# Graph attention over gathered neighbours: lists of the first half made inside layer 1, four tiles in the first phase

## The chip, the cores and the metric

The kernel runs on one core of a Trainium2 chip. Its time is the device time of one execution in microseconds; of several executions the median counts. The core has a matrix engine (TensorE, PE in the profile; its weight loads are PEld), a vector engine (DVE), a scalar engine (ACT), GpSimd (POOL) and SyncE (SP), which issues loads and stores. ACT and POOL issue transfers too. Each engine works its own instructions in order.

## What is computed

Two graph layers over x (4096 x 512) and a sparse weighted adjacency adj (4096 x 4096, symmetric in its pattern, some 0.8% of it above zero, the diagonal among them):

```python
# layer 0
h = max(layernorm(x), 0)
d = rowsum(adj) ** -0.5
x = x + relu((d[:, None] * adj * d[None, :]) @ h @ W0 + b0)
# layer 1
h = max(layernorm(x), 0)
e = leaky_relu((h @ W @ a[:512]) + (h @ W @ a[512:]).T, 0.2)
att = softmax(where(adj > 0, e, -1e12), axis=1)
neg = -softmax(where(adj > 0, -e, -1e12), axis=1)
x = x + elu(concat([att @ h, neg @ h], axis=1) @ wtrans)
```

Layer 0 needs adj as a dense matrix. Layer 1 needs only its pattern, so it works on lists of neighbours.

## The kernel before, in words

**Layer 0, phase 1 (L921 to L983).** Rows come in 32 blocks of 128, columns of the result too. For each row block j the kernel loads the 128 rows of adj for their sums (`load_adj`, L660, four transfers of 512 KB), loads the same rows of the transposed adj for the first group's columns (`load_at`, L840), turns and projects h_j with W0 on PE (`project`, L679, eight PE records of 128x512), scales it by d (L702, ACT) to y_j, and multiplies: `multiply` (L852) adds adj times y_j into one accumulator (a PSUM bank) for every block of `GROUPS[0]`, here six blocks, 26 to 31. A product of floats shows as two PE records. y_j stays in SBUF for the rest of layer 0.

**Layer 0, phase 2 (`group`, L1032).** The remaining 26 blocks follow in groups of four or two, in the order of `GROUPS`. In sixteen steps jp each group loads its part of the transposed adj, makes sums of sub-blocks on DVE (`sum_at`, L880 to L883), and multiplies with seven products in place of eight (`multiply_blocks`, L893, 128x256 records). Within a step stand, in the order in which they are written: the multiply, `pack` (the mask bits of the same columns, ACT L716 or DVE L718, stored to `table` by POOL at L727), `finish0` for a block of the group before (x1, the next layer's h, and eight stores of the row into the eight copies of `table`, most from ACT's queue, L443), and the function `step`, which works off pieces of list making. A group's accumulators are taken over (`evict`, `join_blocks`, L776) at the beginning of the next group.

`EARLY` names groups whose masks are made earlier than the group itself, from columns loaded once more: (24,2) in group 2, (12,4) in group 3, (8,4) in group 4. A group in `EARLY` makes no masks of its own.

**Lists.** For every 64-row block layer 1 needs a list of neighbours: the rows of `table` that are gathered. `make_lists(g)` makes them for one half of the blocks (g=1: blocks 16 to 31, g=0: blocks 0 to 15). `make_keys` (L544) compares flags on DVE, transposes them with eight small PE transposes (L552) and makes keys on DVE. Then come 60 rounds of DVE's max and match_replace (`list_round`, L391, L393), each giving eight more entries; after 21, 39 and 60 rounds a list of one of three classes is complete and DVE turns it into row numbers (`li`, L406). 24 `join`s (L413), eight per class, put them into a DRAM tile with indirect transfers by POOL; all write the same tile, so each waits until the one before has landed. `deal` (L425) loads the finished lists into SBUF in three transfers. The pieces are queued in the Python lists `listing` and `joining`, and `step` takes up to two or three rounds and one join per step. Before, g=1 starts in group 3 and g=0 in group 5, both in layer 0.

**Transition.** The last group (24,2) shares its time with the first pair of layer 1, which starts on rows that are finished by then. `judge` (L1008) compares counts on DVE, and lets a dense version of layer 1 run instead if a list overflowed.

**Layer 1 (`sparse_layer1`).** 32 pairs of 64-row blocks, in the order 16 to 31, then 0 to 15. For each pair POOL gathers 22 tiles of 128 rows (L451; chunks a = 0, 1, 2 with 8, 6 and 8 of them) with the indices that `deal` left. A row holds 512 values of h, one of the scores, and 128 words of mask bits. For each block DVE and ACT make the weights: scores (L463, L469), exp of both signs (ACT, L473), mask (L482), sums (L487 to L493). PE then multiplies (`product`, L1296, 28 records of 128x512), DVE and ACT scale, PE turns (L508), and every second block `finish1` multiplies with wtrans (L1319, 16 records), and adds x1. The loop over k is written out so: product of block k, gathers for a block ahead (chunk 0 for even k, chunks 1 and 2 for odd), weights of block k+2, turn of block k-1, finish of an earlier pair. Tiles of gathered rows have six slots, two pairs' worth, so a gather waits until PE has used the pair two before (POOL g L451 <- PE u L1296 in the waits).

Of the kernel before, what the change touches and what calls it, by code (L numbers as in the profile page):

```python
# [19 lines left out]
P = 128  # L20
IB = 512


GROUPS = ((26, 6), (16, 4), (20, 4), (0, 4), (4, 4), (8, 4), (12, 4), (24, 2))

EARLY = {(24, 2): (2,), (12, 4): (3,), (8, 4): (4,)}
PAIR0 = 16
Y_PARTS = (8, 11, 13)
T_PARTS = (7, 9)
# [230 lines left out]
def gcn_gat_kernel(  # L260
# [251 lines left out]
            nc.scalar.copy(ut[:, g, :, (r % 2) * RB : (r % 2 + 1) * RB], tp[:, :, g, :])  # L512


    late_mask = ctx.enter_context(sbuf(name="late_mask", bufs=1, side="right"))
    late_m = late_mask.tile([P, EJ, TT * P], U8, name="late_m")
    with sbuf(name="y0", bufs=1) as y_pool, sbuf(name="wa", bufs=1) as wa_pool, sbuf(name="bits", bufs=4) as bits_pool, sbuf(name="small0", bufs=4) as small, ExitStack() as rest, ExitStack() as lists:
        list_pool = lists.enter_context(sbuf(name="list", bufs=1, side="right"))
        rank = list_pool.tile([P, EN], F32, name="rank")
        nc.gpsimd.iota(  # L520
            rank, [[-1, EN]], base=EN, channel_multiplier=0, allow_small_or_imprecise_dtypes=True
        )
        before = list_pool.tile([P, NE + 1, NH], F32, name="before")
        nc.gpsimd.memset(before[:, 0, :], 0.0)
        for e in range(NE):
            nc.vector.tensor_tensor(
                before[:, e + 1, :], before[:, e, :], ident[:, e * NH : (e + 1) * NH], ALU.add
            )
        start = list_pool.tile([NH, 1], F32, name="start")
        nc.gpsimd.iota(  # L530
            start, [[0, 1]], base=0, channel_multiplier=STR, allow_small_or_imprecise_dtypes=True
        )
        flags = [list_pool.tile([P, EJ * NE, 2 * NH], BF16, name=f"flags{g}") for g in range(2)]
        keys, lst = {}, {}

        b_bc = wa_pool.tile([P, F], F32, name="b_bc")
# [214 lines left out]
            nc.vector.scalar_tensor_tensor(y, acc, d_all[:, j : j + 1], b_bc, ALU.mult, ALU.add)  # L751
            return y

        def new_y(work, j, k):
            if k < 0:
                return work.tile([P, F], F32, tag="y", name=f"y{j}", bufs=4)
            if k == 0:
                spare.append(make_pool.tile([P, 3, F], F32, tag="keys", name="spare"))
            return spare[0][:, k]

        def evict(i0, acc, work, _):

            return {
                i0 + k: affine(new_y(work, i0 + k, k - 3), a, i0 + k) for k, a in enumerate(acc)
            }

        def join_blocks(i0, n, acc, work, new_w):

            ys = {}
            for x in range(n // 2):  # L770
                p16, p23, p45, p7 = acc[x]
                j0, j1 = i0 + x, i0 + n // 2 + x
                ys[j0], ys[j1] = y, v = [new_y(work, j, -1) for j in (j0, j1)]
                w = new_w(f"w{j0}")[:, :H]
                nc.vector.tensor_copy(y[:, :H], p16[:, :H])
                nc.vector.tensor_tensor(w, p16[:, H:], y[:, :H], ALU.add)  # L776
                nc.vector.tensor_tensor(y[:, H:], p45[:, H:], w, ALU.add)

                def first(p23=p23, y=y):
                    nc.vector.tensor_tensor(y, p23, y, ALU.add)  # L780

                def second(p7=p7, w=w, p45=p45, v=v):
                    two = "p (a f) -> p a f"
                    nc.vector.tensor_tensor(w, p7, w, ALU.add)
                    nc.vector.tensor_tensor(
                        v.rearrange(two, a=2),
                        p45.rearrange(two, a=2),
                        w.unsqueeze(1).to_broadcast([P, 2, H]),
                        ALU.add,
                    )  # L790

                if n == 2:
                    first()
                    affine(y, y, j0)
                    second()
                    affine(v, v, j1)
                else:
                    second()
                    first()
            if n > 2:  # L800
                for j, y in ys.items():
                    affine(y, y, j)
            return ys
# [178 lines left out]
                pack(bits6, i0, j, ats.pop(j), j < 2)  # L982
                mark()  # L983
        pending = (GROUPS[0], partial(evict, i0, acc))
        listing, joining, spare = [], [], []

        def make_lists(g):
            make_keys(g)
# [12 lines left out]
                if r + 1 == CAPS[c] // 8:  # L1001
                    listing.append(partial(rows_and_joins, c))

        def judge():


            ok = small.tile([P, 8], F32, tag="ok", name="ok", bufs=1)
            nc.gpsimd.memset(ok, 1.0)  # L1008
            nc.vector.tensor_tensor(listed, listed, count, ALU.is_equal)
            for g in range(2):  # L1010
                nc.vector.tensor_reduce(ok[:, 4 + g : 5 + g], listed[:, g], AX.X, ALU.min)
            nc.vector.tensor_tensor(room[0], room[0], room[1], ALU.min)
            nc.vector.tensor_scalar(ok[:NH, 0:1], room[0], 0.0, None, ALU.is_ge)
            nc.vector.tensor_reduce(ok[:, 1:2], d_all, AX.X, ALU.min)
            nc.vector.tensor_scalar(ok[:, 1:2], ok[:, 1:2], 0.0, None, ALU.is_gt)
            for g, vec in enumerate((s_all, t_all)):
                sq = small.tile([P, NJ], F32, tag="sq", name=f"sq{g}", bufs=1)
                nc.vector.tensor_tensor(sq, vec, vec, ALU.mult)
                nc.vector.tensor_reduce(ok[:, 2 + g : 3 + g], sq, AX.X, ALU.max)
                nc.vector.tensor_scalar(  # L1020
                    ok[:, 2 + g : 3 + g], ok[:, 2 + g : 3 + g], MAXS * MAXS, None, ALU.is_le
                )
            bad = small.tile([P, 1], F32, tag="bad", name="bad", bufs=1)
            nc.vector.tensor_reduce(bad, ok[:, 0:7], AX.X, ALU.min)
            nc.vector.tensor_scalar(bad, bad, 0.0, None, ALU.is_equal)
            bad_ps = bank("bad_ps")
            nc.tensor.matmul(bad_ps[0:1, 0:1], bad, ones[:, 0:1], start=True, stop=True)
            verdict = const.tile([1, 1], I32, name="verdict")
            nc.vector.tensor_copy(verdict, bad_ps[0:1, 0:1])
            return verdict  # L1030

        def group(b, work, at_pool, sum_pool, step, prod, n_h=2):  # L1032
# [2 lines left out]
            i0, n = GROUPS[b]  # L1035
            nj = 8 // n
            (p0, pn), take = pending
            order = [p0 + k for k in ((0, 2, 1, 3) if b > 1 else range(pn))]
            ats, sums = {}, {}

            def prepare(jp):
# [12 lines left out]
            for jp in range(NP):  # L1054
# [8 lines left out]
                        for x in range(n // 2)  # L1063
                    ]
                multiply_blocks(acc, n, jp, ats[jp], sums[jp])
                if (i0, n) not in EARLY:
                    pack(bits_pool, i0, 2 * jp, ats[jp])
                for (e0, m), when in EARLY.items():
                    if b in when:
# [21 lines left out]
        with sbuf(name="work0", bufs=2) as work, sbuf(name="sums", bufs=3) as sum_pool, sbuf(name="at", bufs=6) as at_pool:  # L1091

            def prod(name):
                return work.tile([P, F], F32, tag="q", name=name, bufs=1)

            for b in range(1, len(GROUPS) - 1):

                def step(jp):
                    if jp == 2 and b in (3, 5):
                        make_lists((1, 0)[b == 5])  # L1100
                    for _ in range((2, 3)[b == 6] if jp != 2 else 0):
                        if listing:
                            listing.pop(0)()
                    if joining:
                        joining.pop(0)()

                group(b, work, at_pool, sum_pool, step, prod)
            while listing:
                listing.pop(0)()
            while joining:  # L1110
                joining.pop(0)()
        lists.close()
        late = ctx.enter_context(sbuf(name="late", bufs=1, side="right"))
        late_h = late.tile([P, n_late, ROW_W], F32, name="late_h")
        ut0 = late.tile([P, 2, FC, P], F32, name="ut0")
        s_pair = late.tile([P, P], F32, name="s_pair")
# [2 lines left out]
        with sbuf(name="work2", bufs=2) as work, sbuf(name="sums2", bufs=2) as sum_pool, sbuf(name="at2", bufs=4) as at_pool, sbuf(name="scratch", bufs=1) as scratch, sbuf(name="pair", bufs=1) as pair:  # L1119
# [94 lines left out]
                        nc.scalar.activation(warm, ones[:, 0:1], AF.Sqrt)  # L1214
                    )

            group(len(GROUPS) - 1, work, at_pool, sum_pool, step, row_tile, 4)
            k = late0 % EJ
            nc.gpsimd.dma_start(
                out=rows_of(tab0, late0 // EJ)[:, k : k + n_late, ROW_W:],  # L1220
# [9 lines left out]
                late_weights0(r)  # L1230
            for r in blocks:
                late_product0(r)
            verdict = judge()


    def sparse_layer1():
        with ExitStack() as pools:

            def pool(name, bufs):
# [3 lines left out]
            slots = ((0, 0), (1, 0), (1, 2), (1, 1), (0, 1), (0, 2))  # L1243
            g_pools = {s: pool("g%d%d" % s, 1) for s in slots}
            tmp, small, p_pool = pool("tmp", 1), pool("small1", 2), pool("p", 3)
            work, ut_pool, wt_pool = pool("work1", 2), pool("ut", 2), pool("wt", 1)
            warm = small.tile([P, 1], F32, tag="warm", name="warm", bufs=1)
            nc.scalar.activation(warm, sign, AF.Exp)
            wt_sb = wt_pool.tile([P, 2 * FC, F], F32, name="wt_sb")
            s_pool = pool("s", 2)  # L1250
            gath, wgt, us, uts, srow = {}, {}, {}, {PAIR0: ut0}, {}

            def load_s(k):
# [106 lines left out]
            for k, r in enumerate(order):  # L1360
# [5 lines left out]
                if k + 4 - k % 2 < len(order):  # L1366
                    for a in ((0,), (1, 2))[k % 2]:
                        gather1(order[k + 4 - k % 2] // 2, a)
                if k + 2 < len(order):
                    weights(order[k + 2])  # L1370
                    if wanted and order[k + 2] % 8 == 7:
# [2 lines left out]
                    turn(order[k - 1])  # L1374
                if k == 2:
                    finish1(PAIR0)
                if k % 2 and k > 1:
                    finish1(order[k - 3] // 2)
            turn(order[-1])
# [43 lines left out]
```

## Time and profile before

| | us |
|---|---|
| median of 3 executions | 2135.89 (2132.7 to 2136.31) |
| the profiled execution, its own time | 2098.72 |
| its span | 2096.8 |
| phase 1, last multiply | 334.3 |
| phase 2, first to last L893 | 334.3 to 1030.2 |
| transition and first blocks of layer 1 | to about 1180 |
| mean granted PE clock | 0.981 |

The groups of phase 2, first to last product on PE (L893), from the trace:

| group | us | |
|---|---|---|
| (16,4) | 98.8 | |
| (20,4) | 97.0 | |
| (0,4) | 107.1 | list rounds, g=1 |
| (4,4) | 115.3 | joins, g=1 |
| (8,4) | 107.5 | list rounds, g=0 |
| (12,4) | 109.0 | joins, g=0 |
| (24,2) | 55.1 | |

In the lines of the profile, times are in us from the span's start unless a column says ns. A line of the groups names the line of the program, the engine, the operation, what it writes and reads, the count, then busy time and mean ns, then the idle time of the engine ahead of it and what ended that. A line of the waits reads: who waited, for whom, us in all, times, longest. "SPq" is SyncE's queue of transfers. In the table by stretches, each engine has its busy us and its number of instructions; PEclk is the granted TensorE clock, DMA share how busy the 16 DMA engines were.

### The profile page before, as it was taken

Reading aid. Unit: us, or ns where it says so; the run is one execution under the profiler, and the core shown is the slowest. Engines: PE = TensorE matmul, PEld = TensorE weight load, DVE = VectorE, ACT = ScalarE, POOL = GpSimd, SP = SyncE. Lnnn points to the kernel's source line nnn. Section 1 sums busy time; section 2 is a strip of 40 time slices with the busy share of each in tenths; the row PEclk is TensorE's granted clock in tenths of the full one; section 3 lists DMA queues with packets and bytes.
Section 4 is the critical chain, followed back from the end, with each engine's and each line's share of the span. In section 5 each row is a group of like instructions: output and inputs, shape, how many; then the busy total and the mean of one; then the engine's idle time right before and its main releaser. Section 6 shows DMA issues by size and latency. Waiting matters only on the chain.

```text
span 2096.8 us, 20037 instructions
## 1 busy us (share of the span) xinstructions
PE 1996.2 (95%) x6456; PEld 1180.1 (56%) x6456; DVE 1120.1 (53%) x2805; ACT 511.3 (24%) x876; POOL 917.0 (44%) x980
## 2 busy tenths in 40 slices
PE   7999999999899879899879999999999999999998
PEld 3444446888787768788634444444444444444443
DVE  5444436563798458945545455554544544445441
ACT  4645612222332310000111222212212211121120
POOL 2010001111113320220577777777777777776740
PEclk9999999999999999999989999999999999999999
DMA  9988927887887776383689888888888888888850
GB/s 381 366 307 321 371 71 252 290 284 220 307 281 256 253 222 238 90 270 111 204 265 302 255 288 293 263 287 254 271 240 274 261 258 245 242 247 236 240 161 22
DMA packets 188040, 524.11 MB, mean 250 GB/s; under 512 B 25235, under 2 KB 34419, under 8 KB 187926
## 3 DMA queue, kind: packets, MB, share of 16 engines
q0 software_dynamic: 71296, 275.22, 42.2%
q1 hardware_dynamic: 86640, 192.78, 27.1%
q10 hardware_dynamic: 29990, 54.75, 7.4%
q8 instruction: 52, 0.85, 0.2%
q14 instruction: 62, 0.51, 0.1%
HBM read 430.83 MB, written 102.92 MB: 255 GB/s over the span
## 4 chain that ended last, share of the span: by engine, by line
PE 49%; DVE 6%; DMA 5%; POOL 3%; issue 2%; ACTq 1%; ACT 0%; DVEq 0%; SPq 0%; POOLq 0%
PE u L1296 32%; PE o L1319 10%; PE p L893 5%; POOL g L451 3%; DMA g<-table,idx 2%; DVE keys L393 1%; PE tp L508 1%; DVE lst L391 1%; DMA table<-h 1%; DMA ld<-li,off 1%; DMA at<-in_adj_t 1%; PE u L1174 1%; ACTq L443 1%; DVE prod L816 0%; DMA table<-m 0%
## 5 line engine op out<-in xcount | busy, mean ns | idle before, releaser
L451 POOL DMA_INDIRECT g<-table,idx x704 | 747.8, 1062 | 259.9 <-issue 186.4
L1296 PE MATMUL u<-g,p 128*128 128x512 f32 x1736 | 762.4, 596 | 9.8 <-DVE p L482 9.8
L1296 PEld LDWEIGHTS u<-g,p 128*128 128x128 f32 x1736 | 326.0, 191 | 397.5 <-issue 362.9
L463 DVE TENSOR_TENSOR z<-g,s 128x512 f32<-128x512 f32 (+1 forms) x124 | 77.5, 625 | 390.4 <-DMA g<-table,idx 357.8
L893 PE MATMUL p<-t,sums 128*128 128x256 f32 x832 | 249.0, 384 | 13.3 <-DVE sums L881 13.3
L893 PE MATMUL p<-y,sums 128*128 128x256 f32 x832 | 252.0, 385 | 6.5 <-DVE sums L883 6.5
L893 PE MATMUL p<-y,at 128*128 128x256 f32 x832 | 252.4, 386 | 4.9 <-DMA at<-in_adj_t 4.6
L1319 PE MATMUL o<-wt_sb,ut 128*128 128x512 f32 x512 | 225.1, 592 | 0.5 <-ACT ut L512 0.5
L473 ACT ACTIVATE p<-z 128x896 f32<-128x896 f32 (+2 forms) x136 | 116.1, 905 | 268.3 <-DVE z L469 248.1
L893 PEld LDWEIGHTS p<-t,sums 128*128 128x128 f32 x832 | 159.6, 193 | 37.5 <-DVE sums L881 15.5
L893 PEld LDWEIGHTS p<-y,sums 128*128 128x128 f32 x832 | 160.7, 193 | 29.9 <-DVE sums L883 7.3
L852 PE MATMUL acc<-y,at 128*128 128x512 f32 x384 | 174.9, 593 | 2.4 <-ACT y L702 2.4
L482 DVE SCALAR_TENSOR_TENSOR p<-g,p 128x384 f32<-128x384 uint8 (+1 forms) x256 | 143.2, 620 | 63.3 <-ACT p L473 62.3
L893 PEld LDWEIGHTS p<-y,at 128*128 128x128 f32 x832 | 159.3, 193 | 30.7 <-ACT m L716 5.0
L727 POOL DMA_DIRECT2D table<-m x71 | 54.3, 766 | 248.5 <-ACT m L716 145.5
L1319 PEld LDWEIGHTS o<-wt_sb,ut 128*128 128x128 f32 x512 | 94.8, 190 | 107.8 <-issue 106.9
L716 ACT ACTIVATE m<-at 128x1024 uint8<-128x1024 f32 (+1 forms) x110 | 105.2, 987 | 183.8 <-DMA at<-in_adj_t 137.3
L893 PE MATMUL p<-t,at 128*128 128x256 f32 x416 | 126.3, 386 | 18.5 <-DVE w L776 17.7
L1305 ACT ACTIVATE us<-u,rl 128x512 f32<-128x512 f32 x62 | 42.5, 686 | 414.7 <-issue 217.4
L679 PE MATMUL yp<-w_sb,hx_t 128*128 128x512 f32 x256 | 123.2, 627 | 17.3 <-ACT y L702 14.8
L852 PEld LDWEIGHTS acc<-y,at 128*128 128x128 f32 x384 | 70.5, 190 | 80.5 <-issue 77.4
L413 POOL DMA_INDIRECT ld<-li,off x48 | 43.2, 901 | 159.8 <-DMA ld<-li,off 115.8
(182 smaller groups left out, 1718.5 us busy)
## 6 DMA issues: line engine op xcount, KB each, us to landing
at<-in_adj_t SPq DMA_DIRECT2D x136, 512.0 KB, 5.1
ar<-in_adj SPq DMA_DIRECT2D x128, 512.0 KB, 8.4
table<-h ACTq DMA_DIRECT2D x182, 258.0 KB, 5.8
table<-m POOLq DMA_DIRECT2D x55, 256.0 KB, 5.6
at<-in_adj_t SPq DMA_DIRECT2D x32, 384.0 KB, 5.0
g<-table,idx POOLq DMA_INDIRECT x704, 4.3
xr<-in_x SPq DMA_DIRECT2D x32, 256.0 KB, 3.5
x<-x1d SPq DMA_DIRECT2D x32, 256.0 KB, 5.2
```

The source lines that it names most:

```text
L413: return nc.gpsimd.indirect_dma_start(out=lst_dram[g][:, :], out_offset=bass.IndirectOffsetOnAxis(ap=off[g][:, e, c : c + 1], axis=0), in_ ...
L451: nc.gpsimd.indirect_dma_start(out=gt[:, k, :], out_offset=None, in_=table[2 * n // RPT], in_offset=bass.IndirectOffsetOnAxis(ap=idx[n // ...
L463: return nc.vector.tensor_tensor(z, t.to_broadcast([P, n, RB]), s.unsqueeze(1).to_broadcast([P, n, RB]), ALU.add)
L473: i = nc.scalar.activation(p[:, :, g, :], z, AF.Exp, scale=(1.0, -1.0)[g])
L482: nc.vector.scalar_tensor_tensor(e, m, 0.0, e, ALU.is_gt, ALU.mult)
L679: nc.tensor.matmul(yp, hx_t[j][:, c * P : (c + 1) * P], w0_sb[:, c, :], start=c == 0, stop=c == FC - 1,)
L716: nc.scalar.activation(m, at, AF.Sign)
L727: nc.gpsimd.dma_start(out=rows_of(t, e)[:, c:, ROW_W + (a - t * TT) * P // 4 : ROW_W + (b - t * TT) * P // 4], in_=masks[i0][:, c:, (a - i ...
L852: nc.tensor.matmul(a, at[:, 0, it * P : (it + 1) * P], y0[j], start=j == 0, stop=j == NJ - 1)
L893: i = nc.tensor.matmul(out, left[:, x * P : (x + 1) * P], right, start=jp == 0 and first, stop=jp == NP - 1 and (final or not first),)
L1296: nc.tensor.matmul(u, p[:, k0 + k].rearrange("p g c -> p (g c)"), gt[:, k, :F].bitcast(F32), start=k0 + k == 0, stop=k0 + k == nk - 1,)
L1319: nc.tensor.matmul(po, ut[:, g, c, :], wt_sb[:, g * FC + c, :], start=g == 0 and c == 0, stop=g == 1 and c == FC - 1,)
```

## The change

Six things, which belong together:

- `GROUPS` begins with (28,4) in place of (26,6): four accumulators in phase 1, and a new group (26,2) in phase 2, third in the order.
- `EARLY` keeps (24,2) alone. The groups (12,4) and (8,4) make their masks from their own columns.
- g=1 is listed in group 4, which is (0,4) as before. g=0 is listed within layer 1: after block k=3 of its loop the memory of the late rows is closed, a pool and the tables for the lists are made, and `make_lists(0)` follows. From k=4 on each k takes five pieces of `listing` and one of `joining`, and one more of `joining` follows each of the gather chunks 0 and 2.
- `judge` stands at k=40 in layer 1.
- The pool of s in layer 1 is made ahead of that of wt, so it lies elsewhere in SBUF. Flags of g=0 have a pool of their own.
- The first group's accumulators are evicted to four y tiles, without the spare tile.

```diff
-GROUPS = ((26, 6), (16, 4), (20, 4), (0, 4), (4, 4), (8, 4), (12, 4), (24, 2))
-
-EARLY = {(24, 2): (2,), (12, 4): (3,), (8, 4): (4,)}
+GROUPS = ((28, 4), (16, 4), (26, 2), (20, 4), (0, 4), (4, 4), (8, 4), (12, 4), (24, 2))
+
+EARLY = {(24, 2): (3,)}
...
-                if (i0, n) not in EARLY:
+                if (i0, n) not in EARLY and 2 * jp % nj == 0:
                     pack(bits_pool, i0, 2 * jp, ats[jp])
...
-                    if jp == 2 and b in (3, 5):
-                        make_lists((1, 0)[b == 5])
-                    for _ in range((2, 3)[b == 6] if jp != 2 else 0):
+                    if jp == 2 and b == 4:
+                        make_lists(1)
+                    for _ in range(2 if jp != 2 else 0):
                         if listing:
                             listing.pop(0)()
...
-            verdict = judge()
...
-            work, ut_pool, wt_pool = pool("work1", 2), pool("ut", 2), pool("wt", 1)
+            work, ut_pool, s_pool, wt_pool = pool("work1", 2), pool("ut", 2), pool("s", 2), pool("wt", 1)
...
-            s_pool = pool("s", 2)
...
                     for a in ((0,), (1, 2))[k % 2]:
                         gather1(order[k + 4 - k % 2] // 2, a)
+                        if a != 1 and joining:
+                            joining.pop(0)()
                 if k + 2 < len(order):
                     weights(order[k + 2])
...
                 if k == 2:
                     finish1(PAIR0)
+
+                if k == 3:
+                    lates.close()
+                    make_pool = pool("make1", 1)
+                    rank, before, start = list_tables(make_pool)
+                    make_lists(0)
+                if k > 3:
+                    for work_left, n in ((listing, 5), (joining, 1)):
+                        for todo in work_left[:n]:
+                            todo()
+                        del work_left[:n]
+                if k == 40:
+                    verdict = judge(small)
```

`list_tables` is the code that made `rank`, `before` and `start` ahead of layer 0 (L519 to L532), now a function that is called a second time.

More of the change, by code (lines that the diff above doesn't have):

```diff
@@ L512, in turn_u @@
             nc.scalar.copy(ut[:, g, :, (r % 2) * RB : (r % 2 + 1) * RB], tp[:, :, g, :])
-    late_mask = ctx.enter_context(sbuf(name="late_mask", bufs=1, side="right"))
+    flag_pools, lates = (ctx.enter_context(ExitStack()) for _ in range(2))
+    flag_pool = flag_pools.enter_context(sbuf(name="flags", bufs=1, side="right"))
+    flags = [flag_pool.tile([P, EJ * NE, 2 * NH], BF16, name="flags0")]
+    late_mask = lates.enter_context(sbuf(name="late_mask", bufs=1, side="right"))
     late_m = late_mask.tile([P, EJ, TT * P], U8, name="late_m")
@@ L518, in gcn_gat_kernel, with list_tables @@
         list_pool = lists.enter_context(sbuf(name="list", bufs=1, side="right"))
[L519 to L527, printed above, removed]
-            )
[L529 to L533, printed above, removed]
+        flags.append(list_pool.tile([P, EJ * NE, 2 * NH], BF16, name="flags1"))
+        def list_tables(pool):
+            rank = pool.tile([P, EN], F32, name="rank")
+            nc.gpsimd.iota(
+                rank,
+                [[-1, EN]],
+                base=EN,
+                channel_multiplier=0,
+                allow_small_or_imprecise_dtypes=True,
+            )
+            before = pool.tile([P, NE + 1, NH], F32, name="before")
+            nc.gpsimd.memset(before[:, 0, :], 0.0)
+            for e in range(NE):
+                nc.vector.tensor_tensor(
+                    before[:, e + 1, :], before[:, e, :], ident[:, e * NH : (e + 1) * NH], ALU.add
+                )
+            start = pool.tile([NH, 1], F32, name="start")
+            nc.gpsimd.iota(
+                start,
+                [[0, 1]],
+                base=0,
+                channel_multiplier=STR,
+                allow_small_or_imprecise_dtypes=True,
+            )
+            return rank, before, start
+        rank, before, start = list_tables(list_pool)
         keys, lst = {}, {}
@@ L752, in affine, with new_y @@
             return y
[L754 to L759, printed above, removed]
+        def new_y(work, j):
+            return work.tile([P, F], F32, tag="y", name=f"y{j}", bufs=4)
         def evict(i0, acc, work, _):
             return {
-                i0 + k: affine(new_y(work, i0 + k, k - 3), a, i0 + k) for k, a in enumerate(acc)
+                i0 + k: affine(new_y(work, i0 + k), a, i0 + k) for k, a in enumerate(acc)
             }
@@ L772, in join_blocks @@
                 j0, j1 = i0 + x, i0 + n // 2 + x
-                ys[j0], ys[j1] = y, v = [new_y(work, j, -1) for j in (j0, j1)]
+                ys[j0], ys[j1] = y, v = [new_y(work, j) for j in (j0, j1)]
                 w = new_w(f"w{j0}")[:, :H]
@@ L984, in gcn_gat_kernel @@
         pending = (GROUPS[0], partial(evict, i0, acc))
-        listing, joining, spare = [], [], []
+        listing, joining = [], []
+        verdict = None
         def make_lists(g):
@@ L1002, in make_lists, with judge @@
                     listing.append(partial(rows_and_joins, c))
-        def judge():
+        def judge(small):
             ok = small.tile([P, 8], F32, tag="ok", name="ok", bufs=1)
@@ L1037, in group @@
             (p0, pn), take = pending
-            order = [p0 + k for k in ((0, 2, 1, 3) if b > 1 else range(pn))]
+            order = [p0 + k for k in ((0, 2, 1, 3) if b > 1 and pn == 4 else range(pn))]
             ats, sums = {}, {}
@@ L1112, in gcn_gat_kernel @@
         lists.close()
-        late = ctx.enter_context(sbuf(name="late", bufs=1, side="right"))
+        late = lates.enter_context(sbuf(name="late", bufs=1, side="right"))
         late_h = late.tile([P, n_late, ROW_W], F32, name="late_h")
@@ L1215, in step @@
                     )
-            group(len(GROUPS) - 1, work, at_pool, sum_pool, step, row_tile, 4)
+            group(len(GROUPS) - 1, work, at_pool, sum_pool, step, row_tile, 3)
             k = late0 % EJ
@@ L1232, in gcn_gat_kernel @@
                 late_product0(r)
-            verdict = judge()
     def sparse_layer1():
+        nonlocal make_pool, rank, before, start, verdict
         with ExitStack() as pools:
```

## The prediction

> **What bounds the kernel now.** I read the page's totals first, then the busy times by stage, then the waits, then single rows of the timeline. The page says that TensorE (PE) is busy nearly throughout, and which groups are concerned:
>
> ```profile
> span 2096.8 us, 20037 instructions
> PE 1996.2 (95%) x6456; PEld 1180.1 (56%) x6456; DVE 1120.1 (53%) x2805; ACT 511.3 (24%) x876; POOL 917.0 (44%) x980
> ...
> L451 POOL DMA_INDIRECT g<-table,idx x704 | 747.8, 1062 | 259.9 <-issue 186.4
> ...
> L413 POOL DMA_INDIRECT ld<-li,off x48 | 43.2, 901 | 159.8 <-DMA ld<-li,off 115.8
> ```
>
> By stage (0 to 334 phase 1; then the groups of layer 0; from 1180 layer 1):
>
> ```profile
> core 0: us, PE busy (x) PEld busy (x) DVE busy (x) ACT busy (x) POOL busy (x), PEclk, DMA share, GB/s
> ...
> 25.00:250.00 225.00, 207.98 (x532) 94.32 (x533) 105.90 (x328) 129.04 (x272) 23.57 (x38) 0.97 0.94 347
> 250.00:334.00 84.00, 84.00 (x217) 37.27 (x216) 32.70 (x85) 22.64 (x40) 3.90 (x7) 1.00 0.40 133
> 334.00:530.00 196.00, 194.22 (x900) 169.84 (x899) 110.76 (x321) 51.18 (x70) 29.90 (x54) 1.00 0.82 271
> 530.00:638.00 108.00, 101.49 (x481) 87.74 (x480) 96.78 (x299) 36.08 (x41) 20.02 (x31) 0.97 0.87 291
> 638.00:753.00 115.00, 101.90 (x450) 87.40 (x449) 61.42 (x171) 31.62 (x37) 38.86 (x50) 0.94 0.77 249
> ...
> 1180.00:2097.00 917.00, 908.25 (x2367) 419.71 (x2365) 431.63 (x799) 182.52 (x308) 623.58 (x587) 1.00 0.78 240
> ```
>
> PE is full where no lists are made (334 to 530) and loses 6 to 13 us per group where DVE makes lists or POOL joins them. Layer 1 loses nothing: PE sets it, POOL (68% busy, plus issue gaps) is second. The waits say who leads whom in phase 1, in the joins and in layer 1:
>
> ```profile
> SPq L840 <- PE acc L852: 116.5, 19, 9.6
> ```
> ```profile
> POOL ld L413 <- DMA ld<-li,off: 115.8, 41, 5.9
> ...
> POOL g L451 <- PE u L1296: 54.9, 47, 3.4
> ```
>
> In phase 1 the load queue waits for PE, not PE for it. A join waits for the landing of the one before. Joins in a quiet stretch (POOL's timeline; the bracket is the idle time before):
>
> ```profile
> 853.87 0.88 POOL L413 DMA_INDIRECT ld<-li,off  x1 [3.14 <-DMA ld<-li,off]
> 857.42 0.83 POOL L413 DMA_INDIRECT ld<-li,off  x1 [2.67 <-DMA ld<-li,off]
> 859.64 0.83 POOL L413 DMA_INDIRECT ld<-li,off  x1 [1.38 <-DMA ld<-li,off]
> ```
>
> And how far layer 1's weights lie ahead of PE: the masks of its sixth block end at 1145.61+2.23=1147.8, the block's product starts at 1158.0.
>
> ```profile
> 1145.61 2.23 DVE L482 SCALAR_TENSOR_TENSOR p<-g,p 128x384 f32<-128x384 uint8 x4 [0.41 <-ACT p L473]
> ```
> ```profile
> 1158.03 2.39 PE L1296 MATMUL u<-g,p 128*128 128x512 f32 x5
> ```
>
> Measured so for every block, this lead is 10 us at block 5, 12 at 6, 17 at 10, 20 at 13, 24 at 19, and stays at 28 from block 23.
>
> **What the Trainium skill says.** "DMA: Bandwidth & Descriptors", Anatomy of one DMA: a POOL-issued DMA has a fixed cost of about 2 us, mostly the confirmation of its write. The trace agrees: joins land 1.9 us after issue at best, 3.3 in the median, 7.1 at worst. "SBUF — State Buffer", Who interferes with whom: a DVE instruction with one SBUF input, outside the two-port modes, doesn't hold up GpSimd. The trace agrees for the list rounds: joins beside L393 take 0.87 us, beside no DVE work 0.85. So I slow no gather for them.
>
> **The change, part by part**, against the profiled execution (2098.72 us, 1.9 more than its span).
>
> 1. *Four accumulators in phase 1.* Issue interval of a 128x512 record 0.43 us, two per product. Per j before: 12x0.433 (multiply) + 8x0.433 (projection) + 0.44 (turn) = 9.1; after: 20 becomes 16 records, 7.37. First multiply at 25.8, last work 3.6: before 25.8+32x9.1+3.6=320.6, measured 334.3, so 13.7 lost on the way. After: 25.8+235.8+3.6=265.2, plus 12 of such losses: **277, −57**. Loads: 87 MB had gone by 250; 4 MB fall away (32 x 128 KB); at 347 GB/s the rest ends near 245, and the last row sum and product follow some 20 later, so transfers are close behind. Bounds 265 to 292, −69 to −42.
>
> 2. *The two blocks more in phase 2.* A group of 4 has 448 records of 0.216 = 96.8 us, the new (26,2) half, **+48.4**. Nominal phase 2 is then 677.6; measured before 695.9 against 629.2, so 67 lost.
>
> 3. *One list fewer in layer 0, and two double loads fewer.* The groups of the second list and its joins took 107.5, 109.0 and 55.1 us: 10.7, 12.2 and 6.7 lost. Without it I leave 4 in each (the first two groups lose 2.0 and 0.2): −18. The first list's groups lost 10.3 and 18.5, the latter with POOL's mask stores queued behind joins, hence ACT and the adj loads; with two double loads of 8.4 MB fewer −10. A stop of 5 at 753 (adj late) goes, the new group loses 2. Losses 67 become 36, **−31**; bounds 15 to 55 (−52 to −12). Parts 2 and 3 together: +17, so layer 0 ends 57−17 = **40 us earlier** (24 to 57).
>
> 4. *Lists in layer 1, PE.* Their 8 transposes (0.5 us) stand on PE behind the product of block 3 and wait for DVE, which reaches the flags' comparison after block 5's weights, at about 1152; PE is there at 1138. PE stands for 14 us. This doesn't add to part 6: POOL's gathers go on meanwhile, and the weights' lead over PE grows by as much, until the buffers hold POOL.
>
> 5. *Lists in layer 1, DVE.* 60 rounds of 0.62+0.68 by the width of the window, with masks, counts and places: 72.8 us by the list of instructions, in blocks 6 to 13, beside 67.4 of their own: 140 in 129 of PE time. The 11 over are covered by the lead (12 to 20) and by part 4's stop: **0**. Without that cover they would be 11.
>
> 6. *Joins on POOL.* 22 gathers per pair at 1.373 = 30.2 us against PE's 32.2: POOL has 2 us to spare per pair, which is all that the lead is made of. The first join waits for its list (L406), ready about 1233 (before's clock); POOL would reach it about 1219: 14. Then 24 joins between gather chunks to the eleventh pair, in runs of 1, 3 and 2, four times over. A lone one 1.2 (0.9 busy and issue gap); a second one waits for the first's landing behind gathers, 5.4 for both; three 7.6: 4x(1.2+7.6+5.4)=57 us. Deals: 3 x 1.27 = 3.8. What is queued behind each join are gathers, for which DVE's scores, then PE wait. 96 gathers at 1.33 (a little less than 1.373, since DVE idles in the stop) end at 1233+57+4+128=1422 instead of 1350: slip 72. Lead there 25: **PE stops +46**. The spare 2 us per pair never give that back, since PE itself is the bound afterwards. Bounds: the twelve joins that follow another at 2.2 (POOL's best spacing; 3.5 above) and the list ready 10 earlier, 46−16−10=20; at 4.9 (spacing in the loaded first list) and the list 12 later, 46+16+12=74.
>
> 7. *The rest.* The verdict's dozen small DVE instructions leave the transition for block 40: −1, hidden there by a lead of 28. s in other memory, the late rows' pools: loads that come blocks ahead, 0 (bounds 0 to +4). Row tables again: 0.6+0.1+0.1 on POOL, in part 6's noise, and 15 small DVE adds among part 5.
>
> Sum: −57+48−31+46−1 = **+5**, on 2098.72 about 2104. The shown median, 2135.89, is 37.2 (1.8%) above the profiled execution; I carry the ratio: 1.0024 x 2135.89 = **2141**. 0.2% (4 us) is about what a measurement of this kernel can tell from no change.
>
> **The rivals.**
> - *R1, joins cost what they cost in the loaded stretch* (landing behind gathers; POOL, blocks 9 to 21). For: DMA share 0.78 here, and at 0.77 (638 to 753) joins were 4.9 apart. Against: within a run no gather is issued. Part 6's upper bound, 74: +33, **2169**.
> - *R2, the joins' stretch on POOL is short*, which ends on the faster side: within a run the queue drains, so each following join lands at the best 1.9 and costs 2.2, and DVE, whose rounds wait for nobody, has the list ready when POOL comes. Part 6's lower bound, 20: −21, **2115**. It decides as soon as the twelve runs and the wait for the list, 57+14=71 in my sum, stay under 62. For: five joins at 872 to 882 stood 2.2 to 2.7 apart. Against: the first of each run lands behind up to eight gathers, whose own landing takes 4.3 in the median.
> - *R3, phase 1 doesn't gain* because transfers take over (0.94 share at 347 GB/s): −42 instead of −57, **2156**. Against: SP's 116.5 us of waiting for PE.
> - *R4, the change doesn't do what it says*: excluded by the instruction order, which shows 256 instead of 384 multiply records and the joins among the gathers.
>
> **How the numbers follow.** As worked out (2128 to 2152): 0.45; of it slower 0.24, same 0.13, faster 0.08. R1 0.20 and R3 0.10, both slower. R2 0.25, faster but for 0.04 of it. So faster 0.29, same 0.17, slower 0.54. Range: half of R1 lies above its 2169 and half of R2 below its 2115; parts 1 and 3 can shift either by their bounds. 2104 to 2174 leaves a fifth out. Forecast 2141.
>
> **What would show it.** Last multiply of phase 1 at 277 (265 to 292). Groups with no lists at 97 to 101 us. Layer 0 done 40 earlier. In layer 1 a PE stop of 14 behind the fourth product; gathers of the eleventh pair 72 later against its PE work, and PE waiting for p, and DVE for g, for 30 to 46 in all around blocks 17 to 21; then none. Wrong would be: joins 4 us and more behind one another in every run (R1), 2.2 (R2), PE in phase 1 waiting for row sums (R3).

## The result, and the profile after

The changed kernel's median is 2149.12 us (six runs, 2148.4 to 2158.68) against 2133.44 for the kernel before, timed beside it: ratio 1.0079, 95% interval 1.0061 to 1.0097. It is slower, by less than 1% but clear of the noise. Repeated later, beside the experiments, it took 2124.43 against 2099.17: 1.0117 (1.0082 to 1.0153). The kernel before itself differs by 1.6% between the two occasions. Which chip the first ran on is not known; a slower and a quicker chip are the likeliest reason, and are meant so below. The first profile of before (2098.72) fits the quicker chip, the first profile of after (2151.41) the slower one, so these two must not be subtracted from each other. Both kernels were therefore profiled again on the quicker chip.

From the page of the first profile after:

```profile
span 2149.5 us, 20394 instructions
## 1 busy us (share of the span) xinstructions
PE 2011.5 (94%) x6554; PEld 1205.5 (56%) x6554; DVE 1131.1 (53%) x2859; ACT 523.2 (24%) x885; POOL 923.1 (43%) x983
...
L451 POOL DMA_INDIRECT g<-table,idx x704 | 752.6, 1069 | 275.1 <-issue 196.9
```

PE has hardly more work (the extra products of (26,2), less those of phase 1), but 53 us more of span. In this profile part of that does not come back when the kernel is repeated: see the last section. The repeated profile of after, by stage:

```profile
core 0: us, PE busy (x) PEld busy (x) DVE busy (x) ACT busy (x) POOL busy (x), PEclk, DMA share, GB/s
...
25.00:240.00 215.00, 202.85 (x538) 92.52 (x539) 108.47 (x349) 134.63 (x284) 19.25 (x32) 0.98 0.94 349
240.00:273.00 33.00, 33.00 (x83) 13.64 (x81) 19.37 (x53) 13.83 (x26) 0.91 (x3) 1.00 0.56 210
...
525.00:629.00 104.00, 100.22 (x477) 86.91 (x476) 95.70 (x299) 20.69 (x25) 18.29 (x29) 0.98 0.62 204
629.00:733.00 104.00, 100.45 (x451) 86.74 (x450) 60.63 (x172) 20.47 (x25) 28.78 (x39) 0.97 0.64 206
733.00:927.00 194.00, 194.00 (x899) 169.88 (x899) 92.35 (x256) 36.09 (x45) 20.18 (x41) 1.00 0.61 205
...
1225.00:1410.00 185.00, 148.59 (x347) 67.66 (x346) 78.23 (x171) 26.30 (x44) 123.17 (x119) 0.88 0.64 193
1410.00:2121.00 711.00, 702.81 (x1832) 324.62 (x1830) 335.16 (x622) 143.11 (x242) 478.51 (x446) 1.00 0.75 235
```

Phase 1 now ends at 273 and keeps the DMA share of 0.94. The groups (8,4) and (12,4), 733 to 927, run with PE full. Then, in layer 1, PE is busy for 149 of 185 us between 1225 and 1410, at 0.88 of the clock: that is where the time comes from. After 1410 nothing is lost.

The two repeated profiles, on one chip (us):

| | before | after | difference | forecast |
|---|---|---|---|---|
| span | 2092.9 | 2121.3 | +28.4 | +5 |
| last multiply of phase 1 | 331.6 | 273.3 | -58.3 | -57 |
| phase 2, first to last product | 695.7 | 714.1 | +18.4 | +17 |
| end of layer 0 | 1027.1 | 987.9 | -39.2 | -40 |
| from there to PE's product of block 20 | 373.0 | 440.3 | +67.3 | +45 |
| from there to the end | 692.8 | 693.1 | +0.3 | 0 |

### The profile page after: what moved, and what is told of

Same layout as the page of the kernel before. It is cut to its first block, busy times and chain, and to the rows that moved or that the text cites. A ratio compares the mean times of both kernels' runs of the same rounds, so it can differ in the third digit from the quotient of the medians.

```text
span 2149.5 us, 20394 instructions
## 1 busy us (share of the span) xinstructions
PE 2011.5 (94%) x6554; PEld 1205.5 (56%) x6554; DVE 1131.1 (53%) x2859; ACT 523.2 (24%) x885; POOL 923.1 (43%) x983
## 5 line engine op out<-in xcount | busy, mean ns | idle before, releaser
L1308 PE MATMUL u<-g,p 128*128 128x512 f32 x1736 | 777.2, 604 | 32.7 <-issue 29.2
L463 DVE TENSOR_TENSOR z<-g,s 128x384 f32<-128x384 f32 (+1 forms) x124 | 77.4, 624 | 406.9 <-DMA g<-table,idx 332.8
L905 PE MATMUL p<-t,sums 128*128 128x256 f32 x896 | 268.6, 384 | 9.9 <-DVE sums L893 8.2
L905 PE MATMUL p<-y,at 128*128 128x256 f32 x896 | 272.3, 386 | 3.9 <-issue 3.4
L905 PE MATMUL p<-y,sums 128*128 128x256 f32 x896 | 271.2, 385 | 2.9 <-issue 2.9
L905 PEld LDWEIGHTS p<-t,sums 128*128 128x128 f32 x896 | 173.0, 193 | 35.8 <-DVE sums L893 10.4
L905 PEld LDWEIGHTS p<-y,at 128*128 128x128 f32 x896 | 171.8, 193 | 31.5 <-issue 6.1
L482 DVE SCALAR_TENSOR_TENSOR p<-g,p 128x384 f32<-128x384 uint8 (+1 forms) x256 | 143.3, 619 | 52.5 <-issue 25.7
L892 DVE TENSOR_TENSOR sums<-at 128x256 f32<-128x256 f32 x112 | 46.8, 418 | 208.5 <-PE p L905 191.9
L864 PE MATMUL acc<-y,at 128*128 128x512 f32 x256 | 120.9, 597 | 7.1 <-ACT y L718 7.1
L685 ACT ACTIVATE ar<-ar 128x1024 f32<-128x1024 f32 x96 | 100.2, 1044 | 12.6 <-DMA ar<-in_adj 12.1
```

Of the source, the lines that this page charges most:

```text
L463: return nc.vector.tensor_tensor(z, t.to_broadcast([P, n, RB]), s.unsqueeze(1).to_broadcast([P, n, RB]), ALU.add)
L482: nc.vector.scalar_tensor_tensor(e, m, 0.0, e, ALU.is_gt, ALU.mult)
L685: i = nc.scalar.activation(ar, ar, AF.Identity, accum_out=part[:, c : c + 1])
L864: nc.tensor.matmul(a, at[:, 0, it * P : (it + 1) * P], y0[j], start=j == 0, stop=j == NJ - 1)
L905: i = nc.tensor.matmul(out, left[:, x * P : (x + 1) * P], right, start=jp == 0 and first, stop=jp == NP - 1 and (final or not first),)
L1308: nc.tensor.matmul(u, p[:, k0 + k].rearrange("p g c -> p (g c)"), gt[:, k, :F].bitcast(F32), start=k0 + k == 0, stop=k0 + k == nk - 1,)
```

## Experiments

All ratios are to the kernel before, timed beside the kernel on the same chip. The kernels up to "joins in runs" ran on one chip, that with ACT's exp moved on a third, the others on a second; the kernel before takes 2099 to 2101 us on each. Where stops of PE are given per block or summed, the time between two products beyond the usual is counted (usual are 0.4 us within a pair and 7.3 us from pair to pair), so slowed instructions between them are in it.

**The kernel before again.** No edit.

> The kernel before, unchanged, for a second profile. The first profiled execution took 2098.72 us, 35 less than the median of the timed runs (2133.4). If the profiled execution was an unusually quick one, this profile has a span near 2131 and shows where the 35 us lie (my guess: stops of PE at group boundaries and at a reduced clock). The rival, that profiling itself makes this kernel quicker, expects 2097 again. Ratio 1.000 +- 0.002.

Measured: 0.9996 (0.9987 to 1.0004), span 2092.9. The span is near the rival's 2097, but not for the rival's reason: the timed runs on this chip agree with it (2101.06), so profiling makes nothing quicker. The 35 us lay between the two occasions, most likely between chips, and not within the kernel.

**Four tiles, with both lists in layer 0.**

```diff
-EARLY = {(24, 2): (3,)}
+EARLY = {(24, 2): (3,), (12, 4): (4,), (8, 4): (5,)}
...
-                    if jp == 2 and b == 4:
-                        make_lists(1)
+                    if jp == 2 and b in (4, 6):
+                        make_lists((1, 0)[b == 6])
...
-                    make_lists(0)
```

> Four tiles in the first phase as in the changed kernel, but both lists in layer 0 with the double loads of before. Theory A (the lists in layer 1 are what costs; four tiles alone are worth phase 1 -60 and the new group +56, about -4 us): ratio to before 0.998 (0.993 to 1.003), and layer 1 at 32.2 us per pair with no stops. Rival B (the four tiles cost, for instance by more stops in phase 2; lists in layer 1 are about even): 1.006 or more.

Measured: 0.9941 (0.9925 to 0.9958). Theory A, at the better end of its span: four tiles alone gain 0.6%. Its groups (4,4), (8,4) and (12,4) take 118.3, 108.0 and 107.9 us; in the changed kernel they take 104.3, 97.4 and 97.4.

**Six tiles, with the first half's list in layer 1.**

```diff
-GROUPS = ((28, 4), (16, 4), (26, 2), (20, 4), (0, 4), (4, 4), (8, 4), (12, 4), (24, 2))
+GROUPS = ((26, 6), (16, 4), (20, 4), (0, 4), (4, 4), (8, 4), (12, 4), (24, 2))
-EARLY = {(24, 2): (3,)}
+EARLY = {(24, 2): (2,)}
...
-                    if jp == 2 and b == 4:
+                    if jp == 2 and b == 3:
```

> The complement: six tiles in the first phase as before, lists of the first half in layer 1 as in the changed kernel, no double loads for (12,4) and (8,4). Theory A: the list's removal from layer 0 gives about 20 to 30 us, its place in layer 1 costs 45 to 85: ratio 1.010 (1.004 to 1.02), and phase 2 about 20 to 30 us shorter than before. Rival B: 0.998 to 1.003.

Measured: 1.0145 (1.0128 to 1.0162). Theory A. (The first group's six accumulators are taken over as in the kernel before.) In its profile phase 2 is 39 us shorter than before, more than expected, phase 1 is 11 longer, for which the runs give no reason, and from the end of layer 0 on it takes 72 us more. The two parts multiply to 0.9941 x 1.0145 = 1.0085, and the changed kernel has 1.0079 and 1.0117. That the parts add up so well is not strong proof, since the unexplained 11 us are in the sum. That the lists in layer 1 are what costs shows after layer 0: 72 us more here, 67 in the changed kernel, 3 in the one with both lists in layer 0.

**The changed kernel again.**

> The changed kernel, unchanged, beside the others on this chip. If the parts add up (four tiles -0.6%, lists in layer 1 +1.45%), the ratio is 1.0086 (1.006 to 1.010). Its first profile holds stretches in which PE and DVE issued an instruction only every 0.7 us, at half the clock, without a wait that the profile shows (974 to 994, 1064 to 1072, 1153 to 1163, 1447 to 1462); none of the profiles of the other kernels has such stretches. If they belong to the chip of that run, they are gone here; if they belong to the change, they are here again.

Measured: 1.0117 (1.0082 to 1.0153), above the expected range, though its interval holds the sum of the parts. The stretches of slow issue are gone. The stops in layer 1 are not.

**No joins in layer 1.**

```diff
-                joining.extend(partial(join, g, li, m) for m in range(c * NE, (c + 1) * NE))
+                if g == 1:
+                    joining.extend(partial(join, g, li, m) for m in range(c * NE, (c + 1) * NE))
...
-        src = lst_dram[g].rearrange("(b n) o -> b (n o)", n=STR)
+        src = lst_dram[1].rearrange("(b n) o -> b (n o)", n=STR)
```

> The changed kernel without the 24 joins of the lists made in layer 1; the deals that follow read the other half's lists, so the second half of layer 1 gathers other rows, in the same number. DVE's rounds, PE's transposes and counts stay. Theory A1 (joins on POOL make the stops of blocks 11 to 20): those stops vanish, ratio to before 0.981 to 0.988. Rival A2 (DVE's rounds make them): 1.000 or more.

Measured: 0.9848 (0.9809 to 0.9888). By stretches, without the joins:

```profile
1097.00:1225.00 128.00, 120.07 (x332) 56.14 (x333) 109.67 (x306) 23.63 (x39) 95.54 (x87) 0.96 0.76 241
1225.00:1410.00 185.00, 185.00 (x481) 85.42 (x480) 104.44 (x208) 41.78 (x68) 144.79 (x133) 1.00 0.86 274
```

PE is full for all 185 us where it had 149, though DVE does all its rounds (110 of 128 us busy just before). What is left are 13 us before block 6. The stops are the joins'.

**No rounds on DVE.**

```diff
-                listing.append(partial(list_round, keys[g], lst[g], n))
+                if g == 1:
+                    listing.append(partial(list_round, keys[g], lst[g], n))
+                elif n == 0:
+                    nc.vector.memset(lst[0], 0.0)
```

> The changed kernel without the 60 rounds of max and match_replace in layer 1 (the list is a constant, its count taken as good; the deals read the other half's lists). The joins stay in their runs. Theory A1: POOL no longer waits for its list but still for the landings, stops of 30 to 45 us stay: ratio 1.000 to 1.008. Rival A2: 0.990 or less.

Measured: 1.0096 (1.006 to 1.0131). That is a little above the expected range, and next to nothing is gained with 60 rounds fewer: in its trace the way from product 9 to product 16 takes 40 us more than in the kernel before, so the stops are still there. Together with the kernel without joins this rules DVE's rounds out.

**One join after each chunk of gathers**, in a fixed order on POOL.

```diff
-                        if a != 1 and joining:
-                            joining.pop(0)()
+                        if joining:
+                            tc.keep_in_program_order(joining.pop(0)())
...
-                    for work_left, n in ((listing, 5), (joining, 1)):
+                    for work_left, n in ((listing, 5),):
...
+            if n != PAIR0:
+                tc.keep_in_program_order(i)
```

> The changed kernel with a single join after every chunk of gathers, in a fixed order on POOL, instead of runs of 1, 3 and 2. Each join's landing then lies under six to eight gathers. Theory A1 (waiting for landings in the runs makes the stops of PE between blocks 11 and 20, 42 us in the trace): ratio to before 0.987 to 0.993, and stops in that stretch under 10 us. Rival A2 (the stops come from DVE's rounds in front of sums and scales, or from the list's lateness): still 1.004 to 1.008.

Measured: 0.9888 (0.9872 to 0.9905). Faster than both kernels. POOL's timeline (idle time before in brackets), first of the changed kernel in its second profile, then of this one:

```profile
1246.66 0.95 POOL L451 DMA_INDIRECT g<-table,idx  x1 [0.30 <-issue]
1247.91 1.10 POOL L413 DMA_INDIRECT ld<-li,off  x1 [0.30 <-issue]
1254.49 0.87 POOL L413 DMA_INDIRECT ld<-li,off  x1 [5.49 <-DVE z L469]
1256.73 0.83 POOL L413 DMA_INDIRECT ld<-li,off  x1 [1.37 <-DMA ld<-li,off]
1257.87 1.00 POOL L451 DMA_INDIRECT g<-table,idx  x1 [0.30 <-issue]
```
```profile
1240.72 0.95 POOL L452 DMA_INDIRECT g<-table,idx  x1 [0.30 <-issue]
1241.97 0.86 POOL L413 DMA_INDIRECT ld<-li,off  x1 [0.30 <-issue]
1243.13 0.97 POOL L452 DMA_INDIRECT g<-table,idx  x1 [0.30 <-issue]
...
1250.71 0.86 POOL L413 DMA_INDIRECT ld<-li,off  x1 [0.30 <-issue]
...
1262.68 1.15 POOL L413 DMA_INDIRECT ld<-li,off  x1 [0.30 <-issue]
```

Counted from the end of one gather to the start of the next, a run of three takes 1257.87-1247.61=10.3 us, a single join 1243.13-1241.67=1.5. (The releaser "DVE z L469" of the second join is the last event by the profile; what it waits for is the landing of the first, 5.8 us after its issue.) The stretch that had the stops:

```profile
1150.00:1450.00 300.00, 299.71 (x781) 138.42 (x780) 187.00 (x427) 59.36 (x99) 234.19 (x217) 1.00 0.80 249
1450.00:1520.00 70.00, 59.18 (x149) 27.16 (x148) 30.26 (x57) 13.09 (x22) 51.43 (x49) 0.93 0.77 243
```

What is left are a stop of 12 us near 1510, where the deals come just ahead of the first gathers that need them, and two at PE's own list work (8.6 and 14.8 us, blocks 4 and 6).

**The same fixed order, but joins in runs.**

```diff
+                        for _ in range((2, 1, 3)[a]):
+                            if joining:
+                                tc.keep_in_program_order(joining.pop(0)())
```

> As the kernel with a single join per chunk, in a fixed order on POOL too, but with runs of 3, 2 and 1 joins after the chunks as the changed kernel has them. Theory A1 (the runs cost): 1.003 to 1.010, stops of 40 to 50 us in blocks 11 to 20. Rival A3 (the fixed order of POOL's queue was the gain, not the spacing): 0.989 again.

Measured: 1.0032 (1.0021 to 1.0044), between the two. The runs cost 1.4% beside single joins (1.0032 to 0.9888, intervals apart), so not the order but the spacing is most of the gain. Spacing means two things here that no run separates: single joins cost POOL less, and they lie among 7.7 pairs' gathers. This kernel does not repeat the changed kernel's pattern either. Each class of lists gives eight joins, and in the trace they come as 1, 3, 2, 1, 1, so that only every second pair has runs. The 24 joins lie among 5.4 pairs' gathers here, among 3.7 in the changed kernel. What it gains on the changed kernel (1.0117 to 1.0032; stops of 34 us in blocks 17 to 24, against 47 and against the 40 to 50 expected) can't be put down to the fixed order alone. Its first join comes 18 us later, without a wait for its list.

The fixed order holds for the gathers too, and that has an effect of its own: counted from the end of layer 0, the first product of the loop (block 0) starts earlier than in the kernel before, by 9 us with single joins and by 12 us here. In the changed kernel it starts 3 us later. PE's stop at its own list work takes this back: at block 6 the changed kernel and the one with single joins are both 13.5 us behind the kernel before. So it isn't what removed the stops of blocks 11 to 20. What the fixed order would be worth in the kernel before was not tried.

**DVE's scores behind the scale of the block in work.**

```diff
+                    with ExitStack() as after:
+                        if r not in first:
+                            after.enter_context(tc.issue_after(scaled[-1].ins))
+                        scores(s, z[:, k : k + n], gt[:, :, ROW_T : ROW_T + 1].bitcast(F32))
```

> The changed kernel, with DVE's scores of block k+2 queued behind the scale (the reciprocal) of block k, so that a wait for gathered rows no longer stands in front of what PE's next step needs. Nothing else changes. Theory C (the lead of about 13 us that is left unused in blocks 11 to 20 can't be used because sums and scales stand behind scores that wait for their gather): PE now stops later and in all some 8 to 12 us less, ratio to before 1.006 to 1.009 against 1.0117. Rival D (the stops are set by the gathers' lateness alone, the order on DVE does not matter): 1.010 to 1.014, with the same stops.

Measured: 1.0039 (1.0028 to 1.005). Better than theory C's range, and clear of rival D's. In the trace product 20 starts 8.7 us earlier than in the changed kernel, counted from the end of layer 0. But 6.6 of them POOL's gathers have too, and the stops that remain in blocks 14 to 20 sum to 44 us. ACT's timeline shows why:

```profile
1279.77 1.79 ACT L473 ACTIVATE p<-z 128x896 f32<-128x896 f32 x2 [27.76 <-DVE z L469]
1281.47 0.67 ACT L1322 ACTIVATE us<-u,rl 128x512 f32<-128x512 f32 x1
```

The scaling that PE's turn waits for stands behind an exp that waits for a later block's rows.

**ACT's exp behind its scaling and copies as well.**

```diff
+                    with tc.issue_after(evicted[-1].ins):
+                        exps(z, p)
```

> From the changed kernel with DVE's scores behind the scale (1.0039), one step more: ACT's exp of block k+2 is queued behind ACT's scaling of block k and its copies of the turn of block k-1, since in that kernel's trace the scaling stood behind an exp that waited 27.8 us for scores. Joins stay in runs. Theory C (what is left of the unusable lead of 8 us is ACT's queue): PE's stops of 44 us in blocks 11 to 20 shrink by a further 5 to 12, ratio 0.998 to 1.002, and the lead of the masks falls under 5 us at the stops. Rival D (the rest is the gathers' lateness): 1.0039 +- 0.002, leads at the stops stay at 8.

Measured: 1.0059 (1.0039 to 1.0079). Theory C was wrong here: no gain over 1.0039, and the ratio lies at the edge of rival D's range. The scale is no longer late, but now PE waits for the sums (PE cs L500 <- DVE total L493: 30.9 us in four stops), since exp, mask and sums start later. Moving a wait out of one queue brought it into another.

**Joins spread over eight pairs' chunks, list work of PE split off.** Four joins per pair; DVE compares flags at block 3, PE transposes at block 5; the places' matmuls wait nine rounds more. The second kernel adds DVE's order from above.

```diff
+            if twice and k == 3 and joining:
+                tc.keep_in_program_order(joining.pop(0)())
...
-                    make_lists(0)
-                if k > 3:
+                    bits0 = make_bits(0)
+                if k == 5:
+                    make_lists(0, bits0)
+                if k > 5:
...
-                if n == 5:
+                if n == (5, 15)[g == 0]:
```

> From the kernel with a single join per chunk: four joins per pair, each with four to eight gathers behind it, so that they end two pairs ahead of the first use; the flags' comparison on DVE two blocks ahead of PE's transposes, and the matmuls of the places nine rounds later. The stops of 8.6 (block 4), 14.8 (block 6) and 12.0 us (block 28) should go or shrink under 4 each: ratio to before 0.977 to 0.982 against 0.9888. If the stops only move (POOL has 2 us to spare per pair and now gives 5 to joins), 0.985 to 0.990.

> The last two edits together. If theory C holds and stops are left in the former, this takes 3 to 8 us off it: 0.974 to 0.980; if none are left, the same within 0.002.

Measured: 0.9926 (0.9904 to 0.9949) and 0.9869 (0.9831 to 0.9907). The first is slower than both of its forecasts. The stops moved: 4.1 us at block 4 and none at 6, but 7.5, 6.3, 1.9, 5.2, 1.2 and 9.2 in blocks 10 to 26, since POOL with four joins per pair needs 30.2+4x1.2=35 us where PE needs 32.2. The second gains 12 us on the first, more than the 3 to 8 expected, though its ratio is above the expected one. Among the kernels that make all of their lists it is the quickest by its median, though not clearly ahead of one join per chunk. Of the 9 us that the fixed order gives at block 0, the first still has 4 and the second 9 at block 6, so part of their time is owed to it.

## Why the prediction was right, and where not

The forecast, 2141 on 2135.89 (1.0024), had the direction; the measured 1.0079 is three times as far from no change. The forecast of +5 us is the small difference of 40 gained and 45 lost, and the bounds on either are far wider than 5 us, so the direction alone could have been luck. The parts show what was understood.

**Parts 1 to 3, layer 0: right.** Phase 1 gained 58 (forecast 57), parts 2 and 3 cost 18 (17). Transfers did not take over (R3): SP's queue now waits for ACT's row sums (61.5 us) and no longer for PE's multiply, but PE lost 273.3-265.2=8 us in phase 1 where 12 were assumed. The groups without lists run in 97.4 us.

**Part 6, POOL's slip: right in size, in part by luck.** The gathers of block 21 end 430.7 us after layer 0 instead of 354.7: 76 late, forecast 72. The list was ready nearly in time (the first join waits 2.5 us, forecast 14). The twelve runs took 63 (57): 24 us of issue and 39 of gaps. The 11 us too many for that wait make up for 8 us too few in part 7. These are lost in the fourth pair, whose first 14 gathers take 26.4 us instead of 18.6, since POOL stands still ahead of the instruction that makes the table `rank` again (second profile after):

```profile
1112.25 0.56 POOL L526 IOTA rank<- 128x512 f32 x1 [7.82 <-issue]
```

Part 7 had 0.6 us for it. POOL stands 7.3 to 9.2 us here in all eleven profiles of kernels that make these tables in layer 1, also in the last kernel, where PE hardly stops at block 4. What POOL waits for the profile doesn't show. Joins that follow another came 2.2 to 6.6 us behind it, 3.9 on average: neither R1's 4.9 nor R2's 2.2; my sum had 3.5.

**The step that failed: "Lead there 25".** The slip was to be reduced by the lead of the masks, 72-25=46 or so. Product 20 is 67 us late, so of the slip of 76 only 9 were covered. Some of the difference is in the lead itself, which at blocks 20 and 21 is 21 to 22 us in the repeated profile of before, where the first has 26 to 27. But 10 to 13 us of it are still there at the stop's end, in blocks 19 to 21 of the changed kernel. The lead of the masks is not a store that can be run down to nothing. From the last gather of a block to its product the kernel before has 30.0 us at block 20. In the changed kernel this distance is 22.8 to 23.1 at the stops before blocks 12, 14, 16 and 18. At block 20, behind the last stop, it is 21.3. So 7 to 9 us could be used, not 25. The rest is needed: landing, scores, exp, masks and sums, and ahead of the product the turn and the finish of the pair before.

Part of it is order. DVE's timeline of the second profile after:

```profile
1260.95 2.22 DVE L482 SCALAR_TENSOR_TENSOR p<-g,p 128x384 f32<-128x384 uint8 x4
1263.20 1.14 DVE L487 TENSOR_TENSOR tree<-p 128x896 f32<-128x896 f32 x1
1271.54 0.69 DVE L463 TENSOR_TENSOR z<-g,s 128x512 f32<-128x512 f32 x1 [7.20 <-DMA ld<-li,off]
1272.15 1.01 DVE L490 TENSOR_TENSOR tree<-tree 128x384 f32<-128x384 f32 x2
1273.19 0.29 DVE L493 TENSOR_TENSOR total<-tree 128x128 f32<-128x128 f32 x1
1283.85 0.56 DVE L463 TENSOR_TENSOR z<-g,s 128x384 f32<-128x384 f32 x1 [10.36 <-DMA g<-table,idx]
```

The sums (L490, L493) of the block that PE wants next stand behind the scores (L463) of a later block, whose rows POOL has not gathered yet. Its masks (L482) were done at 1263.2, and still PE stands from 1271.3 to 1273.5, as its timeline and the waits of 1200 to 1420 show:

```profile
1273.54 0.38 PE L498 MATMUL cs<-ones,total 128*128 128x1 f32 x2 [2.21 <-DVE total L493]
1273.78 13.96 PE L1308 MATMUL u<-g,p 128*128 128x512 f32 x28
```
```profile
DVE z L463 <- DMA g<-table,idx: 75.8, 11, 12.7
...
PE tp L508 <- ACT us L1317: 24.1, 4, 6.9
...
PE cs L498 <- DVE total L493: 12.3, 4, 4.6
```

With DVE's scores moved back the distance falls to 16.3 to 17.8 at the stops before blocks 12 to 18 and to 19.4 at block 20, and product 20 comes 8.7 us earlier. With ACT's exp moved back too it is 19 to 21. So the order accounts for 2 us (block 20) to 7 us (an earlier stop) of the 16 that were missing. That the rest is the chain itself is what the distance suggests; no run isolates it.

**Part 4, PE's stop: right.** Forecast 14, measured 11.6 before block 4, for the flags on DVE. Not to add it was right as well: it is within the 67, which POOL's slip sets. **Part 5: right**, the DVE rounds cost nothing that is seen (1.0096 without them against 1.0117, intervals overlapping; and with the rounds but no joins PE runs full from 1225 to 1410).

**Not in the sum: the clock.** A product right behind such a stop takes 14.0 to 14.3 us instead of 12.3 (13.96 in the lines above), at a granted clock that is 0.88 over the stretch. That is 7 us in four products, part of the 67. The 67.3 consist of 1.9 before block 4, 11.6 there, 46.6 of stops before blocks 11 to 18 (36 of idle time, the rest slow turns and finishes), and these 7.

## What to carry to other kernels

A lead measured between two steps is cover only down to the shortest distance at which the steps can follow each other. Take that distance from the place in the trace where the lead is smallest, and look at what stands between them in each engine's own order. A chain of transfers that wait for each other's landing was cheaper here when they were issued one by one between other work of the same queue. A run of three took 10.3 us, three single ones 4.4; spacing them, in a fixed order and over twice as many pairs, turned a loss of 0.8% to 1.2% into a gain of 1.1%.

## What the hardware showed that was not expected

A stop of PE costs more than its length. The Trainium skill ("TensorE: Matmul & The Clock Gate", Part 1) has a gate that halves the clock of an idle PE and opens after about 3.4 us of sustained work. The trace of the repeated changed kernel agrees: at each of the eight stops between 1225 and 1390, of 2.2 to 6.9 us, the granted share goes to 0.50 and returns 3.2 to 4.8 us after work has begun again, and a product right behind a stop takes 1.7 to 2.0 us more.

The first profile after, which fits the slower chip, has five stretches of some 7 to 15 us in which PE, and in places DVE, issues only every 0.7 us or a multiple of it, mostly with no wait that the profile shows. In four of them PE's clock follows down to a half. The start of the first:

```profile
974.36 0.59 PE L905 MATMUL p<-t,at 128*128 128x256 f32 x2
975.46 0.70 PE L905 MATMUL p<-y,sums 128*128 128x256 f32 x2 [0.50 <-issue]
976.18 0.38 PE L905 MATMUL p<-y,at 128*128 128x256 f32 x1
978.28 0.59 PE L905 MATMUL p<-y,at 128*128 128x256 f32 x1 [1.73 <-issue]
979.71 0.59 PE L905 MATMUL p<-y,sums 128*128 128x256 f32 x1 [0.84 <-issue]
```

None of the other thirteen profiles has them, that of the same kernel on the quicker chip among them. Their cause, and whether they have to do with the 1.6% between the two occasions, stays open.
